# Relations 1 to 3 and the self product of a graph layer: float32 matmuls replaced by float32r products of split operands, with the splits on ScalarE and GpSimd

## The chip, the cores and the metric

The kernel runs on one core of a Trainium2 chip. The metric is device time in microseconds. The kernel before takes 259.1 us, the median of three runs (258.13 to 259.99).

## The reference, cut to what matters

One graph layer with a feed-forward part, on 625 nodes of 512 values; 20625 edges (two directions of 10000, and one loop per node), sorted by destination, each with a type from 0 to 3 and a weight.

```python
h  = relu((x - mean) / sqrt(var + eps))              # 625 x 512
for r in range(4):
    w_r = where(edge_type == r, edge_weight, 0)
    msg += (h[src] @ W_rel[r] + b_rel[r]) * w_r[:, None]
agg = segment_sum(msg, dst) / max(segment_sum(edge_weight, dst), 1)
x1  = layer_norm(h + h @ W_self + b_self + agg) * g1 + b1
ffn = gelu(x1 @ W1 + b_1) @ W2 + b_2                  # 512 -> 1024 -> 512
out = x + layer_norm(x1 + ffn) * g2 + b2
```

## The kernel before, in words

The nodes are cut into five blocks of 125 (NB = 5), each held in a tile of 128 partitions. The program first normalises x block by block on VectorE (`x_stats`, `x_norm`, L624 to L631) and takes 1/sigma by a small power operation on GpSimd (`x_root`, L634). 1/sigma is kept apart in `rx`, since a positive factor passes through the relu. TensorE transposes the blocks, ScalarE copies the result into `hT[i]` (four slices of 128x128 per block).

**The products.** There are five weight matrices: W_rel[0] to W_rel[3] and, as r = R = 4, W_self with the identity added (`added_ident`, L664, so that h + h @ W_self is one product). Each comes in four slices `w_r_k` of 128x512 float32. `product` (L672) multiplies one block by one matrix: four float32 matmuls, which the trace records as two each. So 25 products give the 200 records of L672. Of the products of relations 0 to 3, ScalarE's `evict` (L677) multiplies the PSUM bank by 1/sigma into a kept row tile `m_c`, with c = 5r + i, and SyncE stores that tile to a DRAM `table` (`store_rows`, L336 and L337). The self product is evicted by VectorE into z (`own_row`, L680).

**Two ways to sum over edges.** For blocks 0 to 2 the sums are matmuls: per block there are four units, and in each unit VectorE makes one-hot tiles (`slot_hots`: one L557, one L560, three L562), TensorE multiplies them into four banks of sums (`slot_sums`, 16 small bf16 matmuls, L573), and VectorE empties these (`empty_sums`, four reduces, L579) into `sums_w`. What the hots are made from (`turned`) needs fields that VectorE computes from edge rows which GpSimd fetches by index (`rows_of_windows`, L406). Then `chunk_sum` (L902) multiplies `sums_w` by the 20 kept rows, 20 float32 matmuls per block, 60 in all. For blocks 3 and 4, GpSimd fetches rows of the table by index, 82 indirect DMAs (L783 and L837). They need all 20 rows stored. VectorE adds them (L807, L833) and TensorE sums them (`edge_sum`, L827, L828 and L830, where the first two are float32r matmuls, recorded once each).

**The end.** Per block: layer norm, transposes, the two feed-forward products (`up`, L1004, and `down`, L1013), the second layer norm, the residual, the store.

**The order.** It is not written out. Every piece is an operation given to a class `Plan` with its engine, an assumed duration, what it comes after, which buffers it takes and gives, and a rank. `Plan` places the operations in time by the assumed durations, among those that are ready the one of lowest rank, and the program emits them in that order. Each engine then runs its own list strictly in order, so an operation that waits holds everything behind it on its engine. Where the chip is slower than the plan assumed, the order stays.

Of the kernel before, what the change touches and what calls it, by code (L numbers as in the profile page):

```python
# [136 lines left out]
def gnn_layer(ctx, tc, x, edges, edge_groups, firsts, fourths, windows, w_self, w_rel, w_ffn1, w_ffn2, brel_in, rows_in, cols_in, out, n_edges):  # L137
# [29 lines left out]
    ps = ctx.enter_context(tc.tile_pool(name="ps", bufs=8, space=bass.MemoryType.PSUM))  # L167
    ROWS = 50

# [66 lines left out]
    half = const.tile([P, 1], F32, name="half")  # L236
    nc.vector.memset(half, -0.5)
    gelu_of = const.tile([P, 1], F32, name="gelu_of")
    xw = const.tile([P, 4, INNER], F32, name="xw")
# [26 lines left out]
    def node_constants():  # L266
        place = work.tile([P, 1], F32, tag="place", name="place", bufs=1)
        nc.gpsimd.iota(place, pattern=[[0, 1]], base=0, channel_multiplier=1, allow_small_or_imprecise_dtypes=True)
        nc.gpsimd.memset(node_f, 2.0 * N)
        nc.gpsimd.memset(xw, -1.0)  # L270
# [37 lines left out]
    z = const.tile([P, NB, D], F32, name="z")  # L308
    rx = const.tile([P, NB, 1], F32, name="rx")

# [273 lines left out]

    PARTS = ()
    ORDER = (0, 1, 2, 3, R)
# [12 lines left out]

    plan = Plan(dict(ps=8, add=3, acc=1, one=2, oh=3, low=2, raw=6, row=ROWS - 7, ms=MS, es=6, ow=4, gT=6), free=dict(SP=9.0), behind=0.6)  # L600
    op = plan.op
# [11 lines left out]

    warmed = op("PE", 4.0, warm, rank=(0, 0), take=["ps"], give=["ps", "row"])

# [17 lines left out]
    def x_root(i):  # L633
        nc.gpsimd.tensor_tensor(rx[:, i, 0:1], mv_x[i][:, 2:3], half, op=ALU.pow)  # L634

    for i in range(NB):
# [12 lines left out]
    for n, r in enumerate(ORDER):  # L649
        for k in range(KD):  # L650
            if r == 0:
                w_at[r, k] = op("DMA", 0.0, None, at=W_AT[k])
            else:
                w_at[r, k] = op("SP", 0.95, lambda r=r, k=k: load_w(r, k), take=["raw", "row"], lag=2.2, rank=(1, n))
# [24 lines left out]
    def own_row(i, box):  # L679
        nc.vector.scalar_tensor_tensor(z[:, i, :], box["p"], rx[:, i, 0:1], bself_bc, op0=ALU.mult, op1=ALU.add)  # L680

    own, stored, made_row, used = {}, {}, {}, {}
    for n, r in enumerate(ORDER):
        for i in range(NB):
            box, m = {}, None
            last = i == NB - 1
            for k0, k1 in ((0, 2), (2, 4)) if (r, i) != (0, 0) else ((0, 1), (1, 2), (2, 4)):
                needs = [w_at[r, k] for k in range(k0, k1)] if r != R else [ident_w[k] for k in range(k0, k1)]
                needs += [turned_h[j] for j in turned_h if j[0] == i]
                m = op("PE", 0.86 * (k1 - k0), lambda i=i, r=r, k0=k0, k1=k1, box=box: product(i, r, k0, k1, box),  # L690
                       after=[m, *needs], take=["ps"] if k0 == 0 else [],
                       give=["raw", "raw", "row", "row"] if last else [], rank=(2 if r != R else 2.5, n, i, k0), lag=0.3)
            used[r, i] = m
            if r < R:
                e = made_row[r, i] = op("ACT", 0.69, lambda i=i, r=r, box=box: evict(i, r, box), after=[m, root_x[i]], take=["row"], give=["ps"],
                                        rank=(1, n, i))
                stored[r, i] = op("SP", 0.95, lambda c=r * NB + i: store_rows(c), after=[e], rank=(0.8, n, i), lag=2.5)
            else:
                own[i] = op("DVE", 0.68, lambda i=i, box=box: own_row(i, box), after=[m, bself_at, root_x[i]],
                            give=["ps"] + (["row"] if last else []), rank=(0.6, n, i))  # L700


    made = {}
# [540 lines left out]
```

## Time and profile before

| | |
|---|---|
| median of three runs | 259.1 us (258.13 to 259.99) |
| the profiled execution | 258.33 us |
| its span, first to last recorded instruction | 256.5 us |
| what lies around the span | 1.8 us |
| mean granted TensorE clock | 0.985 of full |
| busy: TensorE | 243.1 us, 95% |
| busy: VectorE | 186.1 us, 73% |
| busy: GpSimd | 126.8 us, 49% |
| busy: ScalarE | 49.2 us, 19% |

In the profile's rows, PE is TensorE's matmuls, PEld its weight loads, DVE is VectorE, ACT is ScalarE, POOL is GpSimd, SP is SyncE. A timeline row gives the start in the span, the duration, both in microseconds, engine, source line, operation, the names out<-in, the shape, and how many instructions the row joins; in square brackets, if there is one, the idle time before it and what ended it. A row of a group gives the count, the busy time in microseconds and the mean of one in nanoseconds, then the idle time before them. Busy shares are means over stages with different limits. The kernel's stages are: to about 30 us normalising and relation 0; from 30 to 116 us products mixed with one-hot sums; from 116 us chunk sums, gathers and the feed-forward part.

### The profile page before, as it was taken

The numbers are of one execution on the slowest core, as the hardware profiler recorded it, in microseconds if no ns is written. First come the engines' busy times: TensorE is split into PE (matmuls) and PEld (weight loads), VectorE is DVE, ScalarE is ACT, GpSimd is POOL, SyncE is SP. The second block draws the span as 40 slices with busy tenths as digits, with TensorE's granted clock in tenths as the row PEclk, the third lists the DMA queues.
The fourth block names the chain that finished last, engine by engine and source line by source line (L and its number), as shares of the span: only waits on it lengthen the run. The fifth ranks groups of instructions, "written<-read, shape, count | busy, mean of one in ns | idle before, by whom it ended". The sixth has DMA issues, their size and how long they took to land. (4 is left out here: it accounts for less than half of the span.)

```text
span 256.5 us, 2860 instructions
## 1 busy us (share of the span) xinstructions
PE 243.1 (95%) x904; PEld 133.4 (52%) x904; DVE 186.1 (73%) x386; ACT 49.2 (19%) x97; POOL 126.8 (49%) x149
## 2 busy tenths in 40 slices
PE   8999989999999899999999999999999997999980
PEld 2554344655645456444444444448854576646950
DVE  4895699999999999769668678787776786023022
ACT  2242232121211111101111201205431121300300
POOL 8386003000000002777778777778777798934401
PEclk9999979999999999999999999999999999999996
DMA  6967812389651211998777676678877640201101
GB/s 141 363 221 236 282 63 49 93 284 291 227 165 40 83 40 46 297 387 270 210 204 217 188 213 188 188 215 288 279 206 211 201 128 1 80 0 40 42 3 44
DMA packets 17967, 43.12 MB, mean 168 GB/s; under 512 B 2990, under 2 KB 3736, under 8 KB 17820
## 3 DMA queue, kind: packets, MB, share of 16 engines
q0 software_dynamic: 7024, 22.27, 29.0%
q1 hardware_dynamic: 10624, 20.37, 24.4%
q10 hardware_dynamic: 300, 0.26, 0.5%
q8 instruction: 8, 0.13, 0.2%
q14 instruction: 11, 0.09, 0.1%
HBM read 36.49 MB, written 6.52 MB: 168 GB/s over the span
## 5 line engine op out<-in xcount | busy, mean ns | idle before, releaser
L783 POOL DMA_INDIRECT ms<-table,row_i x70 | 67.6, 966 | 79.6 <-DMA table<-m 59.2
L672 PE MATMUL pt<-w,hT 128*128 128x512 f32 x200 | 90.8, 604 | 0.0
L672 PEld LDWEIGHTS pt<-w,hT 128*128 128x128 f32 x200 | 37.4, 194 | 40.6 <-issue 39.3
L902 PE MATMUL acc<-m,sums_w 126*128 126x512 f32 x120 | 53.1, 593 | 0.0
L807 DVE SCALAR_TENSOR_TENSOR ea<-ms,wgt_g,ea 128x512 f32<-128x512 f32 x57 | 42.9, 752 | 13.7 <-DMA ms<-table,row_i 13.0
L902 PEld LDWEIGHTS acc<-m,sums_w 126*128 126x128 f32 x120 | 22.5, 190 | 25.7 <-issue 25.4
L1004 PE MATMUL pu<-x1T,w_sb 128*128 128x250 f32 (+1 forms) x192 | 35.6, 341 | 0.0
L1013 PE MATMUL po<-w_sb,gT 128*125 128x512 f32 (+2 forms) x96 | 35.0, 521 | 0.0
L1004 PEld LDWEIGHTS pu<-x1T,w_sb 128*128 128x128 f32 x192 | 31.4, 191 | 4.4 <-issue 1.9
L579 DVE TENSOR_REDUCE sums_w<-bank 126x160 f32<-126x480 f32 x48 | 28.0, 651 | 0.0
L677 ACT ACTIVATE m<-pt,rx 125x512 f32<-125x512 f32 x20 | 13.8, 688 | 66.1 <-PE pt L672 66.1
L1013 PEld LDWEIGHTS po<-w_sb,gT 128*125 128x125 f32 x96 | 16.8, 188 | 16.4 <-issue 13.8
L1031 DVE TENSOR_TENSOR y<-po,z 125x512 f32<-125x512 f32 (+2 forms) x6 | 3.6, 600 | 23.7 <-PE po L1013 23.7
L573 PEld LDWEIGHTS <-w_first 128*128 128x128 bf16 x192 | 13.7, 147 | 8.4 <-DVE w_first L562 4.4
L1008 ACT ACTIVATE gT<-pu,cols 128x250 f32<-128x250 f32 (+1 forms) x24 | 10.3, 436 | 37.0 <-PE pu L1004 37.0
L789 ACT ACTIVATE ea<-ms,ed 128x512 f32<-128x512 f32 x10 | 6.9, 692 | 47.1 <-DMA ms<-table,row_i 35.4
L562 DVE TENSOR_TENSOR w_first<-eqs,turned 128x640 bf16<-128x640 bf16 x36 | 15.5, 487 | 0.4
L573 PE MATMUL bank<-w_first 128*128 128x120 bf16 x192 | 13.9, 225 | 1.3 <-DVE w_first L562 1.1
L557 DVE TENSOR_TENSOR w_first<-turned,grid 128x2000 bf16<-128x2000 bf16 x12 | 14.3, 1195 | 0.0
L837 POOL DMA_INDIRECT ms_first<-table,x_row x12 | 11.4, 949 | 3.7 <-issue 3.4
L299 POOL TENSOR_TENSOR mv_y<-mv_y,half 125x1 f32<-125x1 f32 x5 | 3.2, 646 | 16.9 <-DVE mv_y L294 16.9
L833 DVE SCALAR_TENSOR_TENSOR z<-ms_first,x_on,z 128x512 f32<-128x512 f32 x12 | 9.1, 755 | 2.0 <-DMA ms_first<-table,x_row 1.7
(152 smaller groups left out, 189.5 us busy)
## 6 DMA issues: line engine op xcount, KB each, us to landing
table<-m SPq DMA_DIRECT2D x20, 224.0 KB
w<-in_L_gnn_W_rel_dram SPq DMA_DIRECT2D x16, 256.0 KB
w_sb<-in_L_gnn_W_ffn_dram SPq DMA_DIRECT2D x4, 1024.0 KB
x_late<-in_x_dram SPq DMA_DIRECT2D x1, 1280.0 KB
ms<-table,row_i POOLq DMA_INDIRECT x70, 3.8
w<-in_L_gnn_W_self_dram SPq DMA_DIRECT2D x4, 256.0 KB
late_rows<-in_rows_dram SPq DMA_DIRECT2D x1, 1024.0 KB
out_dram<-y SPq DMA_DIRECT2D x4, 224.0 KB
```

Of the source, the lines that this page charges most:

```text
L557: nc.vector.tensor_tensor(low[:, :, :NG, :], of[:, 0].rearrange("p (a t) -> p a t", t=TB).unsqueeze(2).to_broadcast([P, nb_, NG, TB]), gri ...
L562: nc.vector.tensor_mul(high[:, :, a * HB:(a + 1) * HB, :], eqs, pairs(2 + a))
L573: nc.tensor.matmul(p[:, i * W:(i + 1) * W], low[:, t // TB, :, t % TB], high[:, t // TP, :, t % TP], start=True, stop=True)
L579: nc.vector.tensor_reduce(sums_w[OUTER[d]][:NG + 1, :, n0:n0 + 2 * QT].rearrange("p c (t h) -> p t h c", h=2), p[:NG + 1, :QT * 3 * HB].re ...
L672: nc.tensor.matmul(box["p"], hT[i][:, k, :], raw[r, k], start=(k == 0), stop=(k == KD - 1))
L677: nc.scalar.activation(kept[c][:NG], box["p"][:NG], AF.Copy, scale=rx[:NG, i, 0:1])
L783: nc.gpsimd.indirect_dma_start(out=ms[j], out_offset=None, in_=table[:, :], in_offset=bass.IndirectOffsetOnAxis(ap=row_i[:, j:j + 1], axis=0))
L807: nc.vector.scalar_tensor_tensor(to, ms[j], wgt_g[:, k, q - 1:q], box["sum"], op0=ALU.mult, op1=ALU.add)
L837: nc.gpsimd.indirect_dma_start(out=ms[-b, q], out_offset=None, in_=table[:, :], in_offset=bass.IndirectOffsetOnAxis(ap=x_row[:, b - B0, q: ...
L902: nc.tensor.matmul(acc[b,], sums_w[b][:NG + 1, c, :], kept[c][:NG + 1], start=first, stop=last)
L1004: nc.tensor.matmul(p[:, :self.n], w1_sb[0][:, k, f * P:(f + 1) * P], self.x1T()[:, k, :self.n], start=(k == 0), stop=(k == KD - 1))
L1013: nc.tensor.matmul(p[:at.stop - at.start, :c.stop - c.start], self.gT[f][:, at], w2_sb[0][:, f, c], start=(f == 0), stop=(f == KF - 1))
```

## The change

Relations 1, 2, 3 and the self product (`PARTS = (1, 2, 3, R)`) are no longer float32 matmuls. Both operands are split into a high and a low part, and three products of parts are taken with float32r operands: high by high and low by low into one PSUM bank, and a product of differences into a second bank. The two banks with factors that `rx` now holds in three columns give the product. Relation 0 stays as it is.

- **Splits of h**, five blocks each: `high_h` on ScalarE, `low_h` on VectorE, `diff_h` on GpSimd.
- **Splits of the weights**, 4 matrices by 4 slices: `high_w` on ScalarE, `low_w` on GpSimd, `shift_w` on ScalarE, `diff_w` on GpSimd, each 128x512, in that order for one slice.
- **Products**, 20 of 25: 8 matmuls `product_ends` and 4 matmuls `product_middle` in place of 4 float32 matmuls.
- **Evictions**: for relations 1 to 3 `evict_ends` on ScalarE and then `evict_middle` on VectorE, before the store; for the self product `own_ends` and `own_middle`, both on VectorE.
- **Buffers**: three more row tiles (50 to 53); weight slices in flight at once 6 to 4; the tiles of `diff_h` take the places of `hT` once relation 0 is done.
- **The rank of `slot_hots`** changes from (3, i) to (2, 5i - 32).

`diff_w_dve` is defined and not used. The core of the diff:

```diff
-    PARTS = ()
+    PARTS = (1, 2, 3, R)
...
+    def high_h(i):
+        h_high[i] = row(f"hh_{i}", F32R, (P, KD, P))
+        nc.scalar.activation(h_high[i], hT[i], AF.Copy, scale=HIGH / SHIFT)
+    def low_h(i):
+        h_low[i] = row(f"hl_{i}", F32R, (P, KD, P))
+        nc.vector.scalar_tensor_tensor(h_low[i], h_high[i].bitcast(F32), -SHIFT, hT[i], op0=ALU.mult, op1=ALU.add)
+    def diff_h(i):
...
+        nc.gpsimd.tensor_tensor(h_diff[i], h_high[i].bitcast(F32), h_low[i].bitcast(F32), op=ALU.subtract)
+    def high_w(r, k):
+        w_high[r, k] = row(f"wh_{r}_{k}", F32R)
+        nc.scalar.activation(w_high[r, k], raw[r, k], AF.Copy, scale=HIGH)
+    def low_w(r, k):
+        w_low[r, k] = row(f"wl_{r}_{k}", F32R)
+        nc.gpsimd.tensor_tensor(w_low[r, k], raw[r, k], w_high[r, k].bitcast(F32), op=ALU.subtract)
+    def shift_w(r, k):
+        w_diff[r, k] = row(f"wd_{r}_{k}", F32R)
+        nc.scalar.activation(w_diff[r, k], w_low[r, k].bitcast(F32), AF.Copy, scale=-SHIFT)
+    def diff_w(r, k):
+        nc.gpsimd.tensor_tensor(w_diff[r, k], w_diff[r, k].bitcast(F32), w_high[r, k].bitcast(F32), op=ALU.add)
+    def product_ends(i, r, k0, k1, box):
...
+            nc.tensor.matmul(box["p"], h_high[i][:, k, :], w_high[r, k], start=(k == 0), stop=False)
+            nc.tensor.matmul(box["p"], h_low[i][:, k, :], w_low[r, k], start=False, stop=(k == KD - 1))
+    def product_middle(i, r, k0, k1, box):
...
+            nc.tensor.matmul(box["q"], h_diff[i][:, k, :], w_diff[r, k], start=(k == 0), stop=(k == KD - 1))
+    def evict_ends(i, r, box):
...
+        nc.scalar.activation(kept[c][:NG], box["p"][:NG], AF.Copy, scale=rx[:NG, i, 1:2])
+    def evict_middle(i, r, box):
...
+        nc.vector.scalar_tensor_tensor(kept[c][:NG], box["q"][:NG], rx[:NG, i, 2:3], kept[c][:NG], op0=ALU.mult, op1=ALU.add)
...
         h = op("DVE", 2.75, lambda d=d, u=u, box=box: box.update(hots=slot_hots(d, u)),
-               after=[h, turned_f[d], hot_consts], take=["low"], rank=(3, i))
+               after=[h, turned_f[d], hot_consts], take=["low"], rank=(2, 5 * i - 32))
```

The lists of the engines move at three places. Lines of the changed kernel have other numbers: `low_w` is L716, `diff_h` L708, `diff_w` L723, `evict_middle` L749, `slot_hots` L562 to L567, `empty_sums` L584, `chunk_sum` L1024, the fetch of edge rows L411, of edge groups L505, the gather L905.

First GpSimd, from the last power operation to the first gathers. Before (`rx` is 1/sigma, `rows_first` the edge rows that the fields need, `x_edges` edge groups, `ms` gathered rows):

```order
L634 TENSOR_TENSOR rx_119<-mv_x3_248,half_98 128x1
L634 TENSOR_TENSOR rx_119<-mv_x4_258,half_98 128x1
L406 DMA rows_first_67<-in_windows_dram,at_i_131 128x256 x5
L500 DMA x_edges_107<-in_edge_groups_dram,x_group_106 128x28 x2
L783 DMA ms_92_975<-table_123,row_i_125 128x512
```

GpSimd in the changed kernel, the same place (`wl` are low parts of weight slices, `wd` differences of weights, `hd` differences of h; the name's first two numbers are relation and slice, or the block):

```order
L716 TENSOR_TENSOR wl_1_0_318<-w_1_0_250,wh_1_0_294 128x512
L411 DMA rows_first_67<-in_windows_dram,at_i_132 128x256 x3
L716 TENSOR_TENSOR wl_1_1_363<-w_1_1_264,wh_1_1_322 128x512
...
L708 TENSOR_TENSOR hd_0_406<-hh_0_226,hl_0_232 128x4x128
...
L723 TENSOR_TENSOR wd_1_3_412<-wd_1_3_412,wh_1_3_369 128x512
L411 DMA rows_first_67<-in_windows_dram,at_i_132 128x256 x2
L716 TENSOR_TENSOR wl_2_0_579<-w_2_0_341,wh_2_0_437 128x512
...
L723 TENSOR_TENSOR wd_4_3_1031<-wd_4_3_1031,wh_4_3_1000 128x512
L905 DMA ms_92_1124<-table_124,row_i_126 128x512
```

All 37 operations of 128x512 now stand ahead of the first gather, in runs of up to 12 without a fetch between them, and the fetch of edge rows stands behind the first of them.

Second VectorE, where the last rows of the table are finished. Before, there is nothing of the products of relations 1 to 3 on VectorE. In the changed kernel (`bank` are the PSUM banks of one-hot sums, named by block and unit; `pq` the second bank of a product):

```order
L562 TENSOR_TENSOR w2_first_68<-turned_1_509,grid_115 128x2x1000
L565 TENSOR_TENSOR eqs_117<-turned_1_509,keys_116 128x640
L567 TENSOR_TENSOR w2_first_68<-eqs_117,turned_1_509 128x8x80 x3
L749 SCALAR_TENSOR_TENSOR m_15_892<-pq_3_0_989,rx_119,m_15_892 125x512
...
L584 TENSOR_REDUCE sums_w1_1033<-bank_1_0_0_1034 126x8x20
L749 SCALAR_TENSOR_TENSOR m_19_1012<-pq_3_4_1057,rx_119,m_19_1012 125x512
L584 TENSOR_REDUCE sums_w1_1033<-bank_1_0_1_1040 126x8x20
```

The row `m_19`, the last that the table needs, is finished on VectorE behind the one-hots of five of the 12 units; seven units follow it.

Third TensorE, around the last unit of one-hot sums. Before, it stands among the self products:

```order
L672 MATMUL pt_4_0_931<-w_4_1_632,hT_0_120 128x512
...
L573 MATMUL bank_2_2_3_959<-w2_first_68 128x120
L672 MATMUL pt_4_0_931<-w_4_2_753,hT_0_120 128x512
L672 MATMUL pt_4_0_931<-w_4_3_760,hT_0_120 128x512
...
L573 MATMUL bank_2_3_3_988<-w2_first_68 128x120
...
L672 MATMUL pt_4_1_996<-w_4_0_624,hT_0_120 128x512
```

In the changed kernel it stands among the chunk sums (`acc1`, `acc2` are the sums of blocks 1 and 2, `m_18` and `m_19` kept rows):

```order
L578 MATMUL bank_2_3_3_1514<-w2_first_68 128x120
...
L1024 MATMUL acc1_1370<-m_18_976,sums_w1_1033 128x512
L1024 MATMUL acc1_1370<-m_19_1012,sums_w1_1033 128x512
L1024 MATMUL acc2_1531<-m_0_261,sums_w2_1312 128x512
L1024 MATMUL acc2_1531<-m_1_383,sums_w2_1312 128x512
```

All 25 products and 38 of the 60 chunk sums now precede the last unit of one-hot sums; 22 chunk sums and the feed-forward part follow it.

More of the change, by code (lines that the diff above doesn't have):

```diff
@@ L237, in gnn_layer @@
     nc.vector.memset(half, -0.5)
+    SHIFT = 4096.0
+    HIGH = 1.0 - 2.0 ** -13
     gelu_of = const.tile([P, 1], F32, name="gelu_of")
@@ L598, in gnn_layer @@
     together = [[b, b + 1] for b in range(0, NB - 1, 2)] + [[NB - 1]]
-    plan = Plan(dict(ps=8, add=3, acc=1, one=2, oh=3, low=2, raw=6, row=ROWS - 7, ms=MS, es=6, ow=4, gT=6), free=dict(SP=9.0), behind=0.6)
+    plan = Plan(dict(ps=8, add=3, acc=1, one=2, oh=3, low=2, raw=4, row=1, kept=NC, ms=MS, es=6, ow=6, gT=6, wp=ROWS - 7 - NC - 2 * NB - 5), free=dict(SP=9.0), behind=0.6)
     op = plan.op
@@ L612, in warm @@
             nc.tensor.matmul(p, zeros[:, :P], zeros, start=True, stop=True)
-    warmed = op("PE", 4.0, warm, rank=(0, 0), take=["ps"], give=["ps", "row"])
+    warmed = op("PE", 4.0, warm, rank=(0, 0), take=["ps"], give=["ps", "wp"])
     stats, turned_h, z_made, root_x, mv_x = {}, {}, {}, {}, {}
@@ L653, in gnn_layer @@
             else:
-                w_at[r, k] = op("SP", 0.95, lambda r=r, k=k: load_w(r, k), take=["raw", "row"], lag=2.2, rank=(1, n))
+                w_at[r, k] = op("SP", 0.95, lambda r=r, k=k: load_w(r, k), take=["raw"], lag=2.2, rank=(1, n))
         if n == 1:
@@ new lines, in gnn_layer @@
+    own, stored, made_row, used = {}, {}, {}, {}
+    h_split, w_split, h_pair = {}, {}, []
+    if PARTS:
+        for i in range(NB):
+            t = [turned_h[j] for j in turned_h if j[0] == i]
+            a = op("ACT", 0.69, lambda i=i: high_h(i), after=t, rank=(0.95, 0, i))
+            b = op("DVE", 0.68, lambda i=i: low_h(i), after=[a, *t], rank=(0.85, 0, i))
+            h_pair.append((a, b))
+    ONE = 0.227
+    for n, r in enumerate(ORDER):
+        split = r in PARTS
+        if split:
+            for k in range(KD):
+                w = w_at[r, k] if r != R else ident_w[k]
+                a = op("ACT", 0.69, lambda r=r, k=k: high_w(r, k), after=[w, *(w_split[ORDER[n - 1], q][3] for q in range(KD) if ORDER[n - 1] in PARTS)], take=["wp"], rank=(0.95, n, k))
+                b = op("POOL", 1.27, lambda r=r, k=k: low_w(r, k), after=[a, w], take=["wp"], give=["row" if r == ORDER[-1] else "raw"], rank=(0.8, n, k))
+                d = op("ACT", 0.69, lambda r=r, k=k: shift_w(r, k), after=[b], take=["wp"], rank=(0.9, n, k))
+                c = op("POOL", 1.27, lambda r=r, k=k: diff_w(r, k), after=[d, a], rank=(0.8, n, 10 + k))
+                w_split[r, k] = (a, b, c, d)
@@ L691, in gnn_layer @@
                        after=[m, *needs], take=["ps"] if k0 == 0 else [],
-                       give=["raw", "raw", "row", "row"] if last else [], rank=(2 if r != R else 2.5, n, i, k0), lag=0.3)
+                       give=["wp", "wp"] if last else [], rank=(top, n, 0, i, k0), lag=0.3)
             used[r, i] = m
             if r < R:
-                e = made_row[r, i] = op("ACT", 0.69, lambda i=i, r=r, box=box: evict(i, r, box), after=[m, root_x[i]], take=["row"], give=["ps"],
+                e = made_row[r, i] = op("ACT", 0.69, lambda i=i, r=r, box=box: evict(i, r, box), after=[m, root_x[i]], take=["kept"], give=["ps"],
                                         rank=(1, n, i))
@@ L700, in gnn_layer @@
                             give=["ps"] + (["row"] if last else []), rank=(0.6, n, i))
+    op("DMA", 0.0, None, after=[w_split[R, k][3] for k in range(KD)], take=["wp"] * 4, give=["row"] * 4)
     made = {}
```

60 lines of the change are left out of this document (58 added, 2 removed).

## The prediction

> **What bounds the kernel now.** I read the windows by stage first, then the waits, then the timelines of TensorE, VectorE and GpSimd. The windows (us of the stretch, then busy time of each engine):
>
> ```profile
> 30.00:50.00 20.00, 18.30 (x80) 9.43 (x79) 18.93 (x63) 5.52 (x11) 2.54 (x2) 0.91 0.30 94
> 50.00:100.00 50.00, 48.74 (x236) 25.99 (x235) 49.23 (x90) 7.58 (x11) 0.00 (x0) 1.00 0.48 153
> 116.00:210.00 94.00, 94.00 (x287) 51.76 (x287) 71.90 (x115) 20.76 (x43) 73.25 (x78) 1.00 0.72 216
> ```
>
> The columns behind the stretch are PE, PEld, DVE, ACT, POOL. TensorE is busy all the time, which the mean of 95% also says. But from 30 to 100 us VectorE is busy too: 68.2 of 70 us. GpSimd does nothing from 50 to 100. So in the stage that is changed two engines are full, one is empty, and ScalarE has room (13.1 us in 70). From 116 us on TensorE alone is full.
>
> ```profile
> 101.13 1.15 PE L573 MATMUL bank<-w_first 128*128 128x120 bf16 x16
> 102.12 13.95 PE L672 MATMUL pt<-w,hT 128*128 128x512 f32 x32
> 100.76 0.95 POOL L783 DMA_INDIRECT ms<-table,row_i  x1 [59.22 <-DMA table<-m]
> 206.21 0.95 POOL L783 DMA_INDIRECT ms<-table,row_i  x1 [0.31 <-issue]
> ```
>
> At 101 us three things end nearly together: the last unit of one-hot sums, the last store to the table (GpSimd waited 59.2 us for it), and then four self products. Whatever makes products cheaper shortens the run only if VectorE's one-hots and the table come earlier too.
>
> **Removed: TensorE time.**
>
> ```profile
> 17.12 13.90 PE L672 MATMUL pt<-w,hT 128*128 128x512 f32 x32
> 117.39 0.39 PE L828 MATMUL acc<-el,oh 128*128 128x512 f32 x1
> 117.63 2.74 PE L902 MATMUL acc<-m,sums_w 126*128 126x512 f32 x6
> ```
>
> A float32 product is 8 records at 13.9 / 32 = 0.434, so 3.47 us. A float32r matmul of 128x512 is one record, and the next starts 0.24 after it (117.39 to 117.63). The neighbours of that kind gave 0.22 to 0.24. Twelve of them are 2.6 to 2.9 us; I take 0.23, 2.76. Twenty products save 20 x 0.7 = 14 us of TensorE (11.6 to 16.6).
>
> **Added: GpSimd, ScalarE, VectorE.**
>
> ```profile
> L925 POOL TENSOR_TENSOR x_late<-x_late,late_rows 128x512 f32<-128x512 f32 x5 | 6.2, 1263 | 0.0
> L677 ACT ACTIVATE m<-pt,rx 125x512 f32<-125x512 f32 x20 | 13.8, 688 | 66.1 <-PE pt L672 66.1
> L680 DVE SCALAR_TENSOR_TENSOR z<-pt,rx,bself 128x512 f32<-128x512 f32 x5 | 3.7, 746 | 0.1
> ```
>
> GpSimd gets 16 `low_w`, 16 `diff_w`, 5 `diff_h`: 37 x 1.22 (pace; 1.26 with its own end) = 45 us, all ahead of the first gather in its list, where it had 59 us of nothing. Alone that would fit. ScalarE gets 37 x 0.69 = 25.5 us into a stage in which it was busy 13.1 of 70: cover, and cost only as latency. VectorE gets 5 `low_h`, 15 `evict_middle`, and 5 more evictions of the self product: 25 x 0.66 to 0.75 = 16.5 to 18.8 us, into the stage in which it had 2 us free. What relieves it is that the plan moves seven of twelve one-hot units behind the table.
>
> **What VectorE and GpSimd do to each other.** This decides, and the trace shows it in a few places.
>
> ```profile
> 208.94 1.26 POOL L953 TENSOR_TENSOR z<-z,late_rows 128x512 f32<-128x512 f32 x1
> 210.16 1.26 POOL L1044 TENSOR_TENSOR y<-y,late_rows 125x512 f32<-125x512 f32 x1
> 209.01 2.70 DVE L1041 TENSOR_SCALAR y<-y,mv_y 125x512 f32<-125x512 f32 x1 [0.77 <-POOL mv_y L299]
> 230.91 0.55 DVE L1041 TENSOR_SCALAR y<-y,mv_y 125x512 f32<-125x512 f32 x1 [0.66 <-POOL mv_y L299]
> 207.17 1.27 POOL L950 TENSOR_TENSOR z<-x,late_rows 128x512 f32<-128x512 f32 x1
> 207.49 0.74 DVE L807 SCALAR_TENSOR_TENSOR ea<-ms,wgt_g,ea 128x512 f32<-128x512 f32 x1
> 250.31 0.74 DVE L1050 SCALAR_TENSOR_TENSOR y<-y,mv_y,late_rows 125x512 f32<-125x512 f32 x1
> 250.47 0.98 POOL L299 TENSOR_TENSOR mv_y<-mv_y,half 125x1 f32<-125x1 f32 x1 [9.39 <-DVE mv_y L294]
> 237.20 0.55 POOL L299 TENSOR_TENSOR mv_y<-mv_y,half 125x1 f32<-125x1 f32 x1 [3.05 <-DVE mv_y L294]
> ```
>
> The L1041 takes 0.55 alone and 2.70 when it comes just behind a GpSimd operation: it waits through two of them (208.94 to 211.42) and ends 0.29 later. GpSimd's pair is not slowed. An L807, of which one input is in PSUM, is not slowed either (0.74). And a GpSimd operation of 0.55 takes 0.98 when it starts inside a VectorE operation of two SBUF inputs: it ends 0.40 after that one. So some VectorE work and GpSimd work exclude one another, and a VectorE operation can lose to several GpSimd operations in a row. What is not shown is a one-hot comparison (two inputs in SBUF, bf16) beside a long GpSimd operation, and one row speaks against:
>
> ```profile
> 8.54 0.55 POOL L634 TENSOR_TENSOR rx<-mv_x,half 128x1 f32<-128x1 f32 x1 [2.21 <-DVE mv_x L631]
> 8.67 0.67 DVE L401 TENSOR_TENSOR w_first<-w_first,node_f 128x486 f32<-128x486 f32 x1
> ```
>
> Here neither is slowed, but the GpSimd operation reads one value per partition and may have read it before the other began. The Trainium skill ("SBUF — State Buffer", "Who interferes with whom") has a rule: a VectorE instruction with two SBUF inputs, or in a two-port mode, excludes a GpSimd instruction that reads SBUF, one of them blocking fully; reduces and instructions with one SBUF input don't contend. The 2.70 and the 0.98 agree, the row at 8.67 does not; by that rule rival A below is out and T (below) is not under 92.
>
> **The sum.** I write T for the time at which VectorE finishes `m_19`, the last row of the table, and count what follows it and what precedes it.
>
> ```profile
> 39.53 1.19 DVE L557 TENSOR_TENSOR w_first<-turned,grid 128x2000 bf16<-128x2000 bf16 x1
> 42.37 1.19 DVE L557 TENSOR_TENSOR w_first<-turned,grid 128x2000 bf16<-128x2000 bf16 x1
> 45.25 2.36 DVE L579 TENSOR_REDUCE sums_w<-bank 126x160 f32<-126x480 f32 x4
> L807 DVE SCALAR_TENSOR_TENSOR ea<-ms,wgt_g,ea 128x512 f32<-128x512 f32 x57 | 42.9, 752 | 13.7 <-DMA ms<-table,row_i 13.0
> 33.02 0.56 DVE L467 TENSOR_TENSOR fields<-w_first,fields 128x384 bf16<-128x384 f32 x1
> 15.52 0.15 DVE L631 TENSOR_SCALAR mv_x<-mv_x 128x1 f32<-128x1 f32 x1
> 17.75 1.24 POOL L634 TENSOR_TENSOR rx<-mv_x,half 128x1 f32<-128x1 f32 x2
> ```
>
> After T: one unit of hots is 2.84 us (39.53 to 42.37), its four reduces 2.27 to 2.36. Between `m_19` and the last hots VectorE's new list holds 7 units of hots (19.9), 23 reduces (13.1), 10 evictions of the self product (6.6) and some 20 others, edge adds at 0.66 to 0.75 above all (14): 54 us. TensorE then does the last unit (1) and the rest of its list. Before, its list from the start of the chunk sums to the end of the span took 256.5 - 117.6 = 138.9 us; 38 of the 60 chunk sums now lie ahead of the last unit, 38 x 0.86 = 32.7 us. So 138.9 - 32.7 - 1 = 105 us remain. The span ends at T + 54 + 1 + 105 = T + 160. The gathers don't end later: they can begin some 3 us after T (eviction, store), took 105.4 us before (100.76 to 206.21), and even with all 50.3 us that then followed they give T + 159. So the break-even with the profiled 258.33 is T = 258.33 - 1.8 - 160 = 96.5.
>
> Before T: VectorE is through its x statistics and the first two `low_h` at about 17 (15.67 plus 2 x 0.66). From there to `m_19` its new list holds 58 us: 5 units of hots (14.2), 17 reduces (9.7), 15 `evict_middle` (10.0), 3 `low_h` (2.0), and the chain of fields, degrees and edge columns (22, as in the rows between 15.58 and 48 of before less the idle time). By inputs, 32 of the 58 have all inputs in SBUF, two of them or a plain copy or scaling like L1041, and 26 have one in PSUM or are reduces.
>
> GpSimd is free of `rx` at 19 and has `wl_1_0` at about 20. From there 45 us of splits and the VectorE work that excludes them (27 to 32, some lies before) cannot overlap if that work is excluded: T is at least 20 + 45 + 27 to 32, that is 92 to 97. That is with perfect packing, and the two lists are strings with waits. If GpSimd always wins while it has an operation ready, as at 208.94, the fetch of edge rows is followed by 12 splits in a row (26 to 41 by my walk through the lists); the fields end at 53 and not at 33.6; the first one-hots come at 63, since on TensorE they stand behind `pt_1_4`, whose operands come late too; the ident additions before `low_w` of the self product stand behind hots; and `m_19` comes at 117.6. I take T = 105, between 97 and 117.6: VectorE's short operations do get in whenever GpSimd waits for ScalarE's `shift_w`, but the row at 209.01 shows that they don't alternate. The span is then 265, the execution 266.8; the profiled execution lies 0.8 below the median, so I forecast **267 us**, slower by 8. The likeliest group's own range is 260 to 280.
>
> Small terms: weight slices of relation 3 and the self product now stand behind stores in SyncE's list, since four and not six are in flight. With products later on all paths I count nothing, 1 to 2 us if that cover goes. Gathers beside one-hots may take 1.5 and not 0.95, as here:
>
> ```profile
> 40.01 1.52 POOL L500 DMA_INDIRECT x_edges<-in_edge_groups_dram,x_group  x1 [0.31 <-issue]
> ```
>
> Over seven units that is 4 to 8 gathers by 0.57, at most 5 us, on a path of T + 159 at most.
>
> **Rivals.** *A: the engines don't exclude one another in this work*, or only for moments. The one row at 8.67 speaks for it, 2.70 and 0.98 against. Then VectorE's 58 us run from 17 with 4 to 5 us of waits (for fetched rows at the start, as before, and for products): T = 79 to 80, span 239 to 240, time 242 to 243. This is the other side: it decides as soon as less than half of the 32 us is blocked (T under 96.5). Chance 0.20. *B: they exclude, but pack almost perfectly* because ScalarE's step between `low_w` and `diff_w` opens a gap for each slice: T = 96, time 258.6, no change. Against it stand the runs of up to twelve splits that are ready together. Chance 0.12. *C: GpSimd's strings win throughout*: T = 117.6, span 278, time 280. It is the upper end of my forecast's group, 0.20 of its 0.68. *D: the float32r products run no faster than float32 records*, 0.43 each: TensorE gets 20 x (12 x 0.434 - 3.47) = 35 us more and the run goes well above 280. The 0.24 behind L828 speaks against it; 0.03, within slower.
>
> **How the numbers follow.** Slower: the forecast's group with C and D, 0.68. Same: B, 0.12. Faster: A, 0.20. One per cent, 2.6 us, is about what a measurement of this kernel can tell. Cases of both signs hold much of the chance, so the range reaches from A's 242 to C's 280.
>
> **What would show it.** Right: one-hot comparisons (after's L562) with a mean well over 1.19 where GpSimd splits run, or splits with a mean well over 1.26; reduces and `evict_middle` at 0.57 to 0.75 as ever; the first gather near 108; TensorE with idle time before one-hot sums between 45 and 110, and none after; products at 2.8 us. It is wrong if the first gather comes before 95, or if splits and hots overlap at their old durations; and my sum T + 160 is wrong if TensorE idles after the last unit of one-hot sums.

## The result and the profile after

The changed kernel takes 283.2 us (median of four runs, 281.4 to 285.2), the kernel before 259.5 us on the same chip: 1.092 times as long, 95% interval 1.083 to 1.102. The forecast was 267, range 242 to 280: the direction was right, and 8 us of loss were forecast where 24 came. The profiled execution took 281.97 us, its span is 280.2.

The same windows as in the prediction, now of the changed kernel (PE, PEld, DVE, ACT, POOL behind the stretch; the first number after POOL's is the granted clock):

```profile
30.00:50.00 20.00, 1.88 (x9) 1.22 (x7) 19.59 (x23) 4.09 (x8) 17.26 (x15) 0.63 0.35 103
50.00:100.00 50.00, 40.85 (x218) 32.83 (x219) 46.75 (x93) 17.94 (x33) 19.75 (x16) 0.88 0.36 114
116.00:210.00 94.00, 93.23 (x380) 55.23 (x379) 89.89 (x155) 14.40 (x30) 60.17 (x60) 1.00 0.66 201
```

From 30 to 50 us TensorE did nearly nothing (1.9 us of 20, where it had 18.3), and VectorE was busy all the time, but with 23 instructions and not with 63. So its instructions got longer. What TensorE waited for is the fields, whose transposes come next in its list:

```profile
50.24 0.29 PE L545 MATMUL tf<-ident_b,fields 128*128 128x128 bf16 x1 [18.37 <-DVE fields L465]
```

The granted clock is lower too (0.63 and 0.88 in the first two windows, 0.91 and 1.00 before), but TensorE has waits in both, so the clock alone does not bound them. From 116 us on TensorE is full again.

VectorE's timeline of the changed kernel shows which instructions got longer:

```profile
24.80 6.64 DVE L427 SCALAR_TENSOR_TENSOR before<-at_f,before 128x2 f32<-128x2 f32 x1
33.56 1.28 DVE L531 TENSOR_TENSOR wgt_g<-fl 128x60 f32<-128x60 f32 x1
34.88 1.19 DVE L533 SCALAR_TENSOR_TENSOR w_first<-fl,wgt_g 128x60 f32<-128x60 f32 x1
41.13 1.30 DVE L446 TENSOR_TENSOR w_first<-w_first,rows_first 128x192 f32<-128x192 f32 x1
44.02 5.71 DVE L464 SCALAR_TENSOR_TENSOR w_first<-w_first 128x192 f32<-128x192 f32 x1
51.92 0.56 DVE L472 TENSOR_TENSOR fields<-w_first,fields 128x384 bf16<-128x384 f32 x1
84.21 6.35 DVE L670 TENSOR_TENSOR w<-w,ident 128x128 f32<-128x128 f32 x1
112.78 0.75 DVE L749 SCALAR_TENSOR_TENSOR m<-pq,rx,m 125x512 f32<-125x512 f32 x1 [0.35 <-PE pq L740]
```

The first works on two values per partition and takes 6.64 us; before (L422 there) an instruction of that line took 0.16. Next to it GpSimd's timeline:

```profile
25.19 3.74 POOL L716 TENSOR_TENSOR wl<-w,wh 128x512 fp32r<-128x512 f32 x3
28.88 2.54 POOL L708 TENSOR_TENSOR hd<-hh,hl 128x512 fp32r<-128x512 f32 x2
33.19 4.02 POOL L708 TENSOR_TENSOR hd<-hh,hl 128x512 fp32r<-128x512 f32 x3 [1.77 <-DVE hl L701]
37.18 5.03 POOL L723 TENSOR_TENSOR wd<-wd,wh 128x512 fp32r<-128x512 f32 x4
44.59 4.91 POOL L716 TENSOR_TENSOR wl<-w,wh 128x512 fp32r<-128x512 f32 x4
118.52 1.09 POOL L905 DMA_INDIRECT ms<-table,row_i  x1 [8.15 <-PE pt L733]
243.61 0.95 POOL L905 DMA_INDIRECT ms<-table,row_i  x1 [0.30 <-issue]
```

L427 ends at 31.44, when the five splits from 25.19 end (31.42) and GpSimd has nothing ready. L464 ends at 49.73, L716's row of four at 49.50. The splits in these rows lose next to nothing (1.25 to 1.29 us each). In what follows, a *row* is several GpSimd operations one behind the other. In the row of seven splits from 33.19 to 42.21 VectorE did not wait for the row: seven of its instructions, L531 to L446, took 1.05 to 1.30 us each, and each ended some 0.1 to 0.2 us after the split beside it. They waited for one *turn*, and so did the last one-hots before `m_19` (L567 at 104.82, three in 4.40 us). The splits beside those took up to 1.54 us, so there GpSimd lost time as well. The fields are done at 52.5 (33.6 before), `m_19` at 113.5, the first gather comes at 118.5 (100.8 before), the last at 243.6 (206.2).

Where a time below stands beside 287 to 289 us for the kernel before, the chip ran slowly for either kernel, and only the early part of such a trace and comparisons on that same chip are used.

### The profile page after: what moved, and what is told of

Same layout as the page of the kernel before. It is cut to its first block, busy times and chain, and to the rows that moved or that the text cites. A ratio compares the mean times of both kernels' runs of the same rounds, so it can differ in the third digit from the quotient of the medians.

```text
span 280.2 us, 3178 instructions
## 1 busy us (share of the span) xinstructions
PE 235.4 (84%) x984; PEld 151.3 (54%) x984; DVE 233.6 (83%) x411; ACT 68.3 (24%) x134; POOL 179.6 (64%) x193
## 5 line engine op out<-in xcount | busy, mean ns | idle before, releaser
L905 POOL DMA_INDIRECT ms<-table,row_i x70 | 72.0, 1028 | 29.0 <-issue 17.4
L1024 PE MATMUL acc<-m,sums_w 126*128 126x512 f32 x120 | 54.7, 597 | 0.4 <-DVE sums_w L584 0.4
L1024 PEld LDWEIGHTS acc<-m,sums_w 126*128 126x128 f32 x120 | 21.9, 190 | 23.0 <-issue 21.5
L733 PE MATMUL pt<-wh,hh 128*128 128x512 f32 x80 | 33.6, 420 | 0.0
L734 PE MATMUL pt<-wl,hl 128*128 128x512 f32 x80 | 32.3, 404 | 0.0
L716 POOL TENSOR_TENSOR wl<-w,wh 128x512 fp32r<-128x512 f32 x16 | 20.7, 1313 | 17.2 <-ACT wh L712 8.3
L723 POOL TENSOR_TENSOR wd<-wd,wh 128x512 fp32r<-128x512 f32 x16 | 21.1, 1347 | 13.2 <-ACT wd L720 13.2
L584 DVE TENSOR_REDUCE sums_w<-bank 126x160 f32<-126x480 f32 x48 | 28.6, 647 | 0.0
L740 PE MATMUL pq<-wd,hd 128*128 128x512 f32 x80 | 20.5, 410 | 0.0
L567 DVE TENSOR_TENSOR w_first<-eqs,turned 128x640 bf16<-128x640 bf16 x36 | 18.6, 572 | 0.4
L545 PE MATMUL tf<-ident_b,fields 128*128 128x128 bf16 x15 | 2.5, 305 | 19.5 <-DVE fields L465 18.4
L733 PEld LDWEIGHTS pt<-wh,hh 128*128 128x128 f32 x80 | 16.2, 203 | 3.6 <-PE pt L678 0.2
L734 PEld LDWEIGHTS pt<-wl,hl 128*128 128x128 f32 x80 | 15.9, 199 | 3.5 <-issue 0.2
L678 PE MATMUL pt<-w,hT 128*128 128x512 f32 x40 | 17.7, 592 | 0.0
```

What stands on the lines that cost most here:

```text
L584: nc.vector.tensor_reduce(sums_w[OUTER[d]][:NG + 1, :, n0:n0 + 2 * QT].rearrange("p c (t h) -> p t h c", h=2), p[:NG + 1, :QT * 3 * HB].re ...
L716: nc.gpsimd.tensor_tensor(w_low[r, k], raw[r, k], w_high[r, k].bitcast(F32), op=ALU.subtract)
L723: nc.gpsimd.tensor_tensor(w_diff[r, k], w_diff[r, k].bitcast(F32), w_high[r, k].bitcast(F32), op=ALU.add)
L733: nc.tensor.matmul(box["p"], h_high[i][:, k, :], w_high[r, k], start=(k == 0), stop=False)
L734: nc.tensor.matmul(box["p"], h_low[i][:, k, :], w_low[r, k], start=False, stop=(k == KD - 1))
L740: nc.tensor.matmul(box["q"], h_diff[i][:, k, :], w_diff[r, k], start=(k == 0), stop=(k == KD - 1))
```

## The experiments

**1. GpSimd's splits written, not read.** The lists of all engines stay, GpSimd's time per split stays (1.2 us of writing and a subtraction of one column); it only reads next to nothing. Written out for `low_w` (the kernel has a helper for it):

```diff
-        nc.gpsimd.tensor_tensor(w_low[r, k], raw[r, k], w_high[r, k].bitcast(F32), op=ALU.subtract)
+        nc.gpsimd.tensor_tensor(w_low[r, k][:, 0:1], raw[r, k][:, 0:1], w_high[r, k].bitcast(F32)[:, 0:1], op=ALU.subtract)
+        for _ in range(2):
+            nc.gpsimd.iota(w_low[r, k][:, 1:], pattern=[[1, D - 1]], base=0, channel_multiplier=0, ...)
```

The same for `diff_w` and `diff_h`.

> The changed kernel with its lists of instructions as they are, but low_w, diff_w and diff_h subtract or add one column only and then fill the tile twice with a row of counting numbers, which GpSimd writes and reads from nowhere; so the values of the parts are wrong and the time on GpSimd stays about 1.2 to 1.3 us each. Theory (VectorE's instructions with all inputs in SBUF stand still while GpSimd reads SBUF): the instructions of 5.7 to 6.6 us on VectorE are gone, fields end at about 35 and not 52.5, m_19 at about 80 to 85 and not 113.5, the time is 243 to 255. Rival 1 (the splits are simply a serial chain on GpSimd and ScalarE that is too long for the products): GpSimd's chain is as long as before, m_19 stays at 105 to 114, the time 272 to 283. Rival 2 (VectorE is too full by itself): m_19 at 100 to 110, 265 to 280.

> The changed kernel whose splits on GpSimd are written and not read, as before (wrong values of the parts, the same lists). In its first run m_19 was finished at 82.5 and the first gather came at 86.8, as the theory of exclusion has it (80 to 85; the rivals had 100 to 114). What is open is the time: by exclusion alone, 31 us are given back before the table is finished; 243 to 255 us if the rest of the changed kernel's list stays as long as there (167 us from m_19 to the end), more if the gathers' wait for the layer norm of block 0 (18.9 us here) decides.

In the first run the table was done as the theory said, with `m_19` at 81.8 (the second expectation says 82.5); it took 279.5 us beside 289.2. The second took 251.2 us beside 258.5 for the kernel before (one run, no interval): 32 us less than the changed kernel. Its VectorE timeline:

```profile
24.18 0.16 DVE L427 SCALAR_TENSOR_TENSOR before<-at_f,before 128x2 f32<-128x2 f32 x1
33.32 0.56 DVE L472 TENSOR_TENSOR fields<-w_first,fields 128x384 bf16<-128x384 f32 x1
81.87 0.75 DVE L758 SCALAR_TENSOR_TENSOR m<-pq,rx,m 125x512 f32<-125x512 f32 x1
```

No VectorE instruction is stretched: the fields come at 33.9, `m_19` at 82.6, that is 31 us earlier than in the changed kernel, and the span ends 30.9 us earlier (249.3). Both rivals are out. A chain on GpSimd of the same length is there, and VectorE has the same work. What the change lost, it lost by GpSimd's subtractions, which read SBUF, beside VectorE's work. (The filling instruction is another one than the subtraction; that the reading in it is what matters, and nothing else of it, is argued from this.)

**2. The splits' GpSimd work alone, added to the kernel before.** 37 subtractions that nobody waits for, ahead of the first gather. The one line that differs in the three runs (the remarks behind it are not in the kernels):

```diff
+        nc.gpsimd.tensor_tensor(extra[0], extra[0], extra[1], op=ALU.subtract)   # 2: reads its predecessor's result
+        nc.gpsimd.tensor_tensor(extra[2], extra[0], extra[1], op=ALU.subtract)   # 6: one target tile
+        nc.gpsimd.tensor_tensor(extra[1 + j % 2], extra[0], extra[0], op=ALU.subtract)   # 8: two target tiles in turn
```

> The kernel before with nothing but 37 GpSimd subtractions of 128x512 added ahead of the first gather, on two tiles of their own that nobody waits for (3, 8 and 26 of them in a row, between the fetches). GpSimd was idle from 41.5 to 100.8 us there. Theory: each of them shuts out VectorE's one-hots and fields for its time; of 45 us at least 30 are lost to VectorE, which sets the one-hot sums, so 285 to 300 us, with single VectorE instructions that last as long as a whole row of subtractions (10 us and more). Rival (no exclusion, or the two take turns at once without loss): 259 to 262, and no VectorE instruction over 3 us.

> As the kernel with 37 added subtractions on GpSimd, but each writes to a third tile, so none reads what the one before wrote. There (each reading its predecessor's result) VectorE's instructions with all inputs in SBUF got in one at a time, each ending with a subtraction, about 1.2 to 1.5 us each, and none stood for more than one. Theory (the gap between subtractions that depend on each other lets VectorE in; independent ones keep the port, as in the three instructions of 5.7 to 6.6 us of the changed kernel): VectorE instructions of over 5 us appear, up to the length of a whole row of 8 or 26 subtractions (10 to 33 us), and the subtractions stay at 1.25 us. Rival (the same taking of turns): no VectorE instruction over 2.5 us and subtractions of about 1.5 us in the row of 26.

> The kernel before with 37 added GpSimd subtractions, now writing two tiles in turn and reading a third, so that a subtraction starts before its predecessor is quite finished, as the splits of the changed kernel do (0.04 us early; with one target tile the next started 0.08 us late). Theory (VectorE gets in by that gap; an instruction with all inputs in SBUF that starts during the indirect DMA ahead of a row of overlapping subtractions waits for the whole row): the one-hot instruction that starts during the second fetch of edge groups takes up to 33 us, behind it VectorE has no competitor; time 285 to 300. Rival (turns are taken anyway): none over 2.5 us; 285 to 295 as with one target tile. So the durations tell the two apart, not the time.

The first of the three took 319.4 us beside 289.2, and its trace refutes a part of the theory: VectorE took turns, no instruction lasted over 2.3 us. The second, 292.9 us beside 258.5, did the same up to the first gather, so my reason (reading the predecessor's result) was wrong, or not enough: with one target tile a subtraction still begins 0.08 us after the one before has ended. The third took 295.0 beside 261.9 (one run each). VectorE's timeline in it:

```profile
29.64 7.85 DVE L440 TENSOR_TENSOR w_first<-w_first,node_f 128x192 f32<-128x192 f32 x1
50.15 27.51 DVE L562 TENSOR_TENSOR w_first<-eqs,turned 128x640 bf16<-128x640 bf16 x3
77.58 1.19 DVE L557 TENSOR_TENSOR w_first<-turned,grid 128x2000 bf16<-128x2000 bf16 x1
```

and GpSimd's, where 26 subtractions follow one another:

```profile
50.55 1.05 POOL L655 TENSOR_TENSOR extra_c<-extra_a 128x512 f32<-128x512 f32 x1
51.55 1.04 POOL L655 TENSOR_TENSOR extra_b<-extra_a 128x512 f32<-128x512 f32 x1
75.47 1.03 POOL L655 TENSOR_TENSOR extra_b<-extra_a 128x512 f32<-128x512 f32 x1
```

The next starts 1.00 us after the last, which takes 1.05: they overlap, and one one-hot instruction, the first of the three in the row at 50.15, waits for all 26 of them (26.7 us; 0.49 without). So two things are shown. GpSimd's subtractions cost VectorE its time either way (33 to 34 us over the kernel before; the third run's are shorter, 1.03 to 1.05 us against 1.26 and more, so this is no comparison of turns with rows). And with a moment between the GpSimd operations VectorE waited for one turn everywhere, while without one it can wait for the whole row. It need not: the turns from 33.56 to 41.13 in the changed kernel lie in a row without such moments, and so does an L828 of the third run (19.68 to 21.22), which came between two subtractions.

**3. Pauses in the changed kernel.** A tiny operation behind each split, which reads its result (again written out for `low_w`).

```diff
         nc.gpsimd.tensor_tensor(w_low[r, k], raw[r, k], w_high[r, k].bitcast(F32), op=ALU.subtract)
+        nc.gpsimd.tensor_tensor(paused, w_low[r, k][:, 0:1].bitcast(F32), half, op=ALU.mult)
```

> The changed kernel with one tiny GpSimd multiplication (one value per partition) behind each of the 37 splits, which reads the split's result and so begins only when the split is quite finished; nothing else is changed. With one target tile, where each subtraction waits for the one before, VectorE got in after each; with two tiles it waited for whole rows (27.5 us). Theory (waiting for whole rows is what made m_19 later than with turns): the three instructions of 5.7 to 6.6 us fall to 1.5 to 2.5, fields end at 42 to 48 and not 52.5, m_19 at 100 to 110 and not 113.5, though GpSimd has 7 to 10 us more to do: 270 to 280 us where the changed kernel has 283. Rival (turns or rows, the sum of both engines' work decides): fields later or as late, 283 to 295.

> The changed kernel with a tiny dependent GpSimd multiplication behind each of the 37 splits, a repeat: its first run had the fields at 44.3 and m_19 at 104.7, as the theory has it, but stalls of other origin after 138 us, in the kernel before too, so its time says nothing. Theory (VectorE's waiting for whole rows of splits costs 9 us before m_19, and the rest of the list is as long as in the changed kernel, 167 us from m_19 to the end): 272 to 277 us. Rival (the table comes earlier but something else ends the run): 279 to 283.

> The changed kernel with pauses between its splits, this time beside the changed kernel itself on one chip. Theory: m_19 at 103 to 106, and 6 to 11 us less than the changed kernel. Rival: within 3 us of it.

> The changed kernel once more, as the measure for the one with pauses: m_19 at 112 to 115, 281 to 286 us where the kernel before takes 259, in proportion more where that takes more. Both theories expect the same of it.

In all three runs `m_19` was done at 104.4 to 105.8. VectorE in the third:

```profile
24.46 1.69 DVE L427 SCALAR_TENSOR_TENSOR before<-at_f,before 128x2 f32<-128x2 f32 x1
44.83 0.56 DVE L472 TENSOR_TENSOR fields<-w_first,fields 128x384 bf16<-128x384 f32 x1
103.63 0.74 DVE L757 SCALAR_TENSOR_TENSOR m<-pq,rx,m 125x512 f32<-125x512 f32 x1
```

The instruction that took 6.64 us takes 1.69; the fields come 7 us earlier, `m_19` 9 us, although GpSimd has 37 operations more to do. The changed kernel beside it had `m_19` at 113.1. The four times with pauses were 294.2 to 298.7 us, the four of the changed kernel 300.5 to 314.8, beside 288.3 for the kernel before. So the pauses help, by 6 us if the lowest of each are compared; the size is known no better than that. The two earlier runs took 302.4 beside 287.4 and 298.6 beside 287.3 (1.038 times as long, 1.025 to 1.051). They had no changed kernel on their chips, and the 1.092 cannot be set against them: on the third run's chip the changed kernel's lowest time was only 1.05 times the lowest of the kernel before.

**4. Three other parts, with less work on GpSimd or none.** High by high, high by low, low by high in one bank; low by low is left out, and with it fall the differences, `shift_w` and the second evictions. First with `low_w` on GpSimd (16 operations), then on VectorE (none).

```diff
+            nc.tensor.matmul(box["p"], h_high[i][:, k, :], w_low[r, k], start=False, stop=False)
+            nc.tensor.matmul(box["p"], h_low[i][:, k, :], w_high[r, k], start=False, stop=(k == KD - 1))
...
-        nc.gpsimd.tensor_tensor(w_low[r, k], raw[r, k], w_high[r, k].bitcast(F32), op=ALU.subtract)
+        nc.vector.tensor_sub(w_low[r, k], raw[r, k], w_high[r, k].bitcast(F32))
```

> The changed kernel with another set of parts for the same 20 products: high by high, high by low and low by high, all three with float32r operands into one PSUM bank (low by low is left out), no tiles of differences, so 16 GpSimd operations and not 37, no second eviction on VectorE, and as many one-pass matmuls (12) per product. One-hot units stand earlier in the order: 15 of 60 chunk sums ahead of the last unit. Theory: GpSimd shuts VectorE out for at most 20 us, so the last one-hots come at 104 to 124 and the end 126 us later: 232 to 252, most likely 245, faster than before since TensorE's 14 us are then nearly all saved. Rival (any GpSimd work in this stage costs more than the passes save): 259 or more.

> The kernel with high by high, high by low and low by high (low by low left out), 16 operations on GpSimd. Fields come at about 46 (one row of four subtractions stops VectorE for 5.7 us, another 4 us), last one-hots at about 105 to 115, 126 us of TensorE behind them: 232 to 250, most likely 243. Rival: 259 or more if TensorE waits again behind its one-hots.

> The same three products, with low_w on VectorE: no added work on GpSimd but the five tiny rescalings, 16 more instructions of 0.68 us on VectorE (10.6 us), which no longer loses to anybody. 31 of 60 chunk sums ahead of the last one-hots. Theory: VectorE is through the last one-hots at 115 to 125, TensorE is the bound with 243 - 14 us of work and few waits: 238 to 250, most likely 244, and no VectorE instruction over 2.4 us before 110. Rival (VectorE's 10.6 us cost as much as GpSimd's exclusion): slower than the one with 16 operations on GpSimd by 5 or more.

With 16 operations: 263.2 us, 1.018 (1.011 to 1.025) times the kernel before, which I had expected to be beaten (the first run took 291.7 beside 289.2). With none on GpSimd and 16 more on VectorE: 246.1 us, 0.951 (0.945 to 0.957). The rows of VectorE with the 16 operations, and then the groups without:

```profile
24.68 3.97 DVE L427 SCALAR_TENSOR_TENSOR before<-at_f,before 128x2 f32<-128x2 f32 x1
31.03 5.69 DVE L446 TENSOR_TENSOR w_first<-w_first,rows_first 128x192 f32<-128x192 f32 x1
```

```profile
L562 DVE TENSOR_TENSOR w_first<-turned,grid 128x2000 bf16<-128x2000 bf16 x12 | 14.4, 1196 | 0.0
L567 DVE TENSOR_TENSOR w_first<-eqs,turned 128x640 bf16<-128x640 bf16 x36 | 15.5, 487 | 0.4
L716 DVE TENSOR_TENSOR wl<-w,wh 128x512 fp32r<-128x512 f32 x16 | 10.1, 686 | 0.0
```

Two rows of three and four splits, early, hold the fields back (41.4 instead of 33.9), and TensorE waits 7.44 us for them (2.46 in the other version). TensorE's waits make some 8 of the 17 us between the two versions; the rest is not traced. On VectorE the same 16 operations cost 10.1 us, and nothing is stretched (487 and 1196 ns as before the change). That is the version that beats both kernels: TensorE's windows in it are nearly full,

```profile
30.00:50.00 20.00, 17.18 (x75) 13.64 (x76) 18.90 (x61) 7.54 (x15) 2.54 (x2) 0.83 0.37 110
50.00:100.00 50.00, 49.53 (x304) 40.24 (x303) 47.66 (x95) 10.35 (x16) 11.86 (x12) 1.00 0.62 192
```

and the span is 12.2 us shorter than before, of the 14 that the passes save.

**5. The gathers' wait.** In the changed kernel GpSimd's list has the power operation of block 0's layer norm between two gathers:

```profile
139.65 0.95 POOL L905 DMA_INDIRECT ms<-table,row_i  x1 [0.30 <-issue]
152.96 0.57 POOL L303 TENSOR_TENSOR mv_z<-mv_z,half 128x1 f32<-128x1 f32 x1 [12.36 <-DVE mv_z L298]
```

```diff
-        s = op("DVE", 0.95, lambda b=b: block_stats(b), after=adds[b], rank=(0.4, b))
+        s = op("DVE", 0.95, lambda b=b: block_stats(b), after=adds[b], rank=(0.4, b), lag=15.0 if b == 0 else 0.08)
```

The longer lag moves it 12 gathers later in the plan.

> The changed kernel with one operation placed otherwise: GpSimd's power operation for the layer norm of block 0 stands 12 gathers later in its list, where it no longer waits 12.4 us for VectorE; the transposes of that block are later too. Theory (gathers decide the end by some 3.5 us of TensorE's last idle time): the last gather comes about 12 us earlier, the end 2 to 5 us earlier, 278 to 281 us where the changed kernel has 283; not more, since TensorE is busy behind the last one-hots anyway. Rival 1 (gathers alone set the end): 270 to 272. Rival 2 (they set nothing): 283.

> The changed kernel with the power operation for the layer norm of block 0 twelve gathers later in GpSimd's list (a repeat beside a usual kernel before). Theory (the gathers' wait for VectorE decides 2 to 5 us of the end): 278 to 281 where the changed kernel has 283. Rival 1 (gathers alone set the end): 270 to 272. Rival 2 (they set nothing): 283.

> The three products with low_w on VectorE, and that power operation twelve gathers later. There TensorE was busy from 42 us to the end of the chunk sums without a wait, and GpSimd waited 7.3 us for the power operation. Theory (TensorE is the bound there, not the gathers): no change from 246, 244 to 248. Rival (gathers decide there too): 239 to 243.

The first run took 319.5 us beside 289.2. The second took 279.3 us beside 261.9: 1.070 (1.061 to 1.079) where the changed kernel has 1.092. The profiled span was 276.9, 3.3 less than 280.2. That is the expected 2 to 5 us by the spans; by ratios it would be 5.7, and the intervals leave both open. But the edit did not do what it was meant to: the last gather came at 240.6, 3 us earlier and not 12, since GpSimd now waited at the power operation of the next block.

```profile
171.42 0.57 POOL L303 TENSOR_TENSOR mv_z<-mv_z,half 128x1 f32<-128x1 f32 x1 [11.89 <-DVE mv_z L298]
```

And 1.1 of the 3.3 us were there before the moved operation, with `m_19` at 112.4. So what the gathers' wait costs is not settled by this run. On the version with nothing on GpSimd the edit changed nothing (0.951 both times; 249.4 us beside 261.9): there TensorE is the bound.

## Why the prediction was wrong in size

- **Bound, and what is removed: right.** A product of 12 matmuls runs at 0.227 to 0.23 us each (starts at 28.76, 28.99, 29.22), 2.75 us, as taken. The version without GpSimd's splits got 12 of the 14 us.
- **Costs of the added operations: right.** GpSimd 1313 to 1347 ns, VectorE's second eviction 742, ScalarE 621 to 625 (0.69 was taken). Evictions from PSUM and reduces were not stretched: L749 stays at 742 and L584 at 647 ns (651 before). A copy or scaling with one input in SBUF can be, as the prediction counted it: L367 at 20.20 took 1.27 us beside a split, where the same instruction of the kernel before took 0.33.
- **Exclusion: right, and it is the cause.** Experiment 1 shows it with the lists unchanged. The row at 8.67 that spoke against it was weak evidence, as the prediction itself says: its GpSimd partner reads almost nothing. Rival A is what happens when GpSimd doesn't read: it gave `m_19` at 79 to 80 and 242 to 243 us, experiment 1 had 82.6 and 251.2.
- **T = 105: this step failed**, by 8.5 us. The sentence was that VectorE's short operations do get in whenever GpSimd waits, so I took a value between perfect packing (97) and waiting for whole rows (117.6). Both turns and rows occur: L531 and others took turns, L427, L464 and L670 waited for rows, 18.7 us in three instructions that take 0.8 without. With pauses, which leave only turns, `m_19` comes at 104.4. So the 105 was near the time of a kernel that takes turns only, though the pauses also add work, which makes the nearness partly chance. The row at 209.01 had already shown a wait through two operations in a row; I had read it as a sign only.
- **Rival C came out nearest in its numbers** (117.6 for `m_19`, 280 us; measured 113.5 and 281.97 in the profiled execution), but partly by luck. Its rows did not win throughout, its T is 4 us too late, and that and the next error, which has the other sign, largely cancel. I gave it 0.20 and let the range end at it.
- **T + 160: the second failed step**, by 6.7 us (280.2 less 113.5 is 166.7). The one-hots after T took 55.1 and not 54 us, their sums on TensorE ended at 170.7, 2.1 us later and not 1, and 109.5 us followed, not 105. In these 109.5 TensorE waited 4.2 us (0.40, 0.25, 0.66 and the two below), where its list of the kernel before, from the chunk sums on, had one wait of 2.0; the sign that the prediction named for a wrong T + 160 came true. "The gathers don't end later" was an error too: I carried over their 105.4 us, but they took 125.1 (118.52 to 243.61), with 12.4 us of waiting for a VectorE result that the one-hots now precede, and they began 5.0 us after T, not 3. TensorE's last block waited for them:

```profile
256.18 0.66 PE L308 MATMUL tp_x<-ident,x 128*128 128x128 f32 x4 [2.31 <-DVE x L1061]
257.39 8.81 PE L1126 MATMUL pu<-x1T,w_sb 128*128 128x125 f32 x64 [0.55 <-ACT x1T L1069]
```

  In experiment 5 it was 164.5 from `m_19` to the end, 2.2 less; how much of the 6.7 us the gathers make stays open. Experiment 1 has the same 166.7, so this part doesn't depend on the exclusion.
- **Checks that I named.** First gather near 108: came at 118.5. TensorE idle before one-hot sums and not after: so it was before 110 us (18.4 us before the transposes of the fields, 6.5 and 3.6 before sums), but afterwards there were the 4.2 us above. Mean of the one-hot comparison L562 well over 1.19: wrong, it is 1190 ns; the small instructions of the fields and the L567 (572 for 487) lost the time, since the big ones mostly fell where GpSimd had nothing ready.
- **SyncE and weight slices: counted at nothing**, and little shows against it: ScalarE waited once, 2.0 us before 34.27, for a weight slice, inside TensorE's 18.4 us of waiting for the fields. ScalarE's longest wait for an input of the splits was another, 8.8 us for the ident addition on VectorE, the L670 above.

## What to carry to other kernels

An idle engine is not free time for its neighbour if both read SBUF: before giving elementwise work to GpSimd, list what VectorE does in the same stretch with all inputs in SBUF, and count it as serial. If it must be there, leave gaps between GpSimd's operations (putting VectorE's urgent chain ahead of them may help too, but no run here shows it); better, put the work on the busier engine that doesn't collide (10.1 us on VectorE cost less than 20 on GpSimd). And a list that carries waits of another path (the power operation between gathers) has to be walked again when that path moves.

## What was not expected of the hardware

A VectorE instruction of two values per partition took 6.6 us, and a one-hot instruction 26.7, beside GpSimd operations that overlap by 0.03 to 0.05 us; with 0.08 us between them (one target tile was enough) VectorE waited for one. The Trainium skill ("SBUF — State Buffer", "Who interferes with whom") says that the one that starts first has the port pair for its whole instruction and the other fully blocks; that agrees for the instructions that took turns. The runs add that the blocked one may not get the pair at that instruction's end. And L427 and L464 had started before the first split of their rows (24.80 for 25.19, 44.02 for 44.59) and were blocked all the same, which the rule does not explain. What decides between one turn and a row where the splits overlap is not settled: in the changed kernel the instructions that waited for rows had started during an indirect DMA of GpSimd or within 0.1 us of the first split (24.80, 44.02, 84.21), those that took turns later in a split (33.56). But in the third run of experiment 2 the L440 started 0.4 us into a subtraction, as L531 did into a split, and waited for eight, and the L828 started 0.06 us into the first of two and waited for one.

A GpSimd subtraction of 128x512 with both inputs from one tile took 1.04 us, with two tiles 1.26 (experiment 2).
